# A place of its own for every step of a planned adapter kernel, and fourteen more W1 blocks by DMA

## The chip, the cores and the metric

The kernel runs on one core of a Trainium2 chip. The core has five engines, each with its own in-order queue: PE (TensorE, matrix products; its weight loads are listed as PEld), DVE (VectorE), ACT (ScalarE), POOL (GpSimd) and SP (SyncE, which here only issues DMAs). The metric is the device time of one execution in microseconds (us); less is better.

## The reference

128 batches of 128 x 512 floats, each with an id of one of ten "languages". A batch takes its own weights by its id, and passes through a small adapter, a layer norm and a residual:

```python
w1 = W1[ids]                                    # 512 x 128 per batch
w2 = W2[ids]                                    # 128 x 512
h = relu(einsum('bsh,bha->bsa', x, w1) + b1[ids])
y = x + einsum('bsa,bah->bsh', h, w2) + b2[ids]
normed = (y - mean(y)) * rsqrt(var(y) + 1e-5)
out = x + normed * gamma[ids] + beta[ids]
```

Everything is float32.

## The kernel before

W1 and W2 of all languages, and b2, gamma and beta spread over the 128 partitions, are loaded or made once at the start. After that each batch b passes through these steps, each a function of its own:

- SP: `load_x` (four batches in one DMA of 1 MB, four buffers, so sixteen batches), `store` (two batches, 512 KB). SP waits at a DMA until its data or its buffer is ready, with everything behind it in the queue.
- PE: `transpose_x` (four transposes, into the one PSUM buffer pxT), `down` (four products with W1, into the one PSUM buffer ph), `up` (the product with W2, into one of the five PSUM buffers py).
- ACT: `copy_xT` (pxT to SBUF), `stage_w1` (copies the batch's W1 from the loaded table), `relu` (ph to hT), `square` (sum of squares of py), and per pair of batches `scalar_means` and `deviation` (the root; L426).
- POOL: `add_b2` (r = x + b2) and `add_beta` (o = x + beta, in one of eight buffers of two batches).
- DVE: `residual` (py = py + r, with its sum), per pair three small Newton steps `rstd`, then `scale` (times gamma) and `finish` (o = py * rstd + o). The finish frees the buffer of py.

Batches differ in two ways. A letter of KINDS says how b2 and x get in. P: r is made by POOL. E ("seeded"): ACT copies x into py beforehand (`seed`), the product is added onto it (L367), and DVE adds b2 from its table; POOL then has one add less. "-" stands for the older forms in the first and last batches (b2 by a product, or by an extra DVE add). A letter of TURNS says how W1 and the transposed x come. T: by `stage_w1` and `transpose_x`. w: W1 by id from HBM (`load_late`, a DMA of 256 KB in pieces of 512 bytes), x by `transpose_x`. F: both in 32 x 32 blocks by DMA (`load_rows`, `load_blocks`), turned on DVE (`turn_blocks`, L302); such a batch has no `transpose_x` and no `copy_xT`.

The order of all this is a plan: each step of each batch is put down with a due time, in units of a batch, and the plan is sorted. Before, the due times are b plus one offset per step (BATCH, PAIR), with a second set (BATCH_EDGE, EDGE) for the "-" batches. KINDS and TURNS repeat every sixteen batches, KINDS from batch 26 and TURNS from batch 32 on. The sorted order becomes the order of each engine's queue; `keep` ties every instruction behind the one before it on its engine. Buffers are handed out in the sorted order too, the one that was freed longest ago first. The opening up to `x_turn(4)` stands ahead of the plan; the last steps (E is 123: products from batch 119 on, finishes from 116 on) are written out by hand behind it and use the same functions.

Of the kernel before, what the change touches and what calls it, by code (L numbers as in the profile page):

```python
# [22 lines left out]
U = 2  # L23
MIDDLE = 26
TURNED = 32
LAST = 4
# [5 lines left out]
BATCH_EDGE = dict(copy=0.2, r=0.05, r_late=1.05, beta=1.06, relu=1.3, w1=-0.6, up=2.5)  # L32
SEED = {'E': 1.69}
PAIR = dict(stat=0.22, square=0.34, means=1.98, root=1.9, scale0=3.03, n1=2.43, n2=3.115, n3=3.28, scale1=3.4, end0=3.67, end1=4.32)
EDGE = dict(stat=0.6, square=0.68, means=1.75, root=1.77, scale0=2.64, n1=2.65, n2=3.592, n3=3.62, scale1=3.64, end0=3.66, end1=4.66)
# [3 lines left out]
def cond_resid_kernel(ctx: ExitStack, tc: tile.TileContext, x, itok, W1, b1, W2, b2, gamma, beta, out):  # L39
# [225 lines left out]
    def b2_by_matmul(b):  # L265
        return b in (0, 1) or b >= B - 2

    def kind(b):
        return KINDS[b % len(KINDS)] if MIDDLE <= b < B - LAST else "-"

    def turn(b):
        return TURNS[b % len(TURNS)] if TURNED <= b < B - LAST - 2 else "-"

# [3 lines left out]
    def b2_on_gpsimd(b):  # L277
        return kind(b) in ON_GPSIMD or kind(b) == "-" and not b2_by_matmul(b) and not b2_by_vector(b)

    def b2_by_vector(b):  # L280
        return kind(b) == "-" and (b in (2, 3, 9, 13, 17, 21) or 24 <= b < B - 8 and (b % 16 in (1, 6, 11) or b % 32 == 30))
# [127 lines left out]
    def square(b):  # L409

        g, j = divmod(b, 2)
        if j == 0:
            ssqs[g] = st.tile([P, 2], FP, tag="ssq", name=f"ssq_{g}")
# [236 lines left out]

    for b in range(B):
        when = BATCH_EDGE if kind(b) == "-" else BATCH
        if b >= 20 and b % G == 0:
            at((11 if b == 20 else b - 7) - 0.01, load_x, b // G)
# [4 lines left out]
        if turn(b) in "Fw":  # L659
            at(b + BATCH["load"] - 1, lid, b, ET.SP)  # L660
            at(b + BATCH["load"], load_rows if turn(b) == "F" else load_late, b)
        if turn(b) == "F":
            at(b + BATCH["load"], load_blocks, b)
            at(b + BATCH["turn"], turn_blocks, b)
        elif 5 <= b <= E - 2:
            at(b, transpose_x, b)
            at(b + when["copy"], copy_xT, b)
        if 4 <= b <= E - 3:
            at(b + (when["r"] if seeded(b) else when["r_late"]), add_b2, b)
            at(b + when["beta"], add_beta, b)  # L670
            at(b + 1.1, down, b)
            at(b + when["relu"], relu, b)
        if seeded(b):
            at(b + SEED[kind(b)], seed, b)
        if FIRST <= b <= E - 1 and turn(b) not in "Fw":
            at(b + when["w1"], stage_w1, b)
        if 2 <= b <= E - 4:
            at(b + when["up"], up, b)
# [4 lines left out]
    def at_pair(g, when, step, *args):  # L683
        if g < E // 2 - 3 or (step, *args) in begun:
            at(2 * g + 3 + when, step, *args)

    for g in range(E // 2 - 1):
        b = 2 * g
        when = EDGE if "-" in (kind(b), kind(b + 2)) else PAIR
        for j in (0, 1):  # L690
            at_pair(g, j + when["stat"] - 0.01, vector_b2, b + j)
            at_pair(g, j + when["stat"], residual, b + j)
            at_pair(g, j + when["square"], square, b + j)
        at_pair(g, when["means"], scalar_means, g)
        at_pair(g, when["root"], deviation, g)
        if b % G == 0 and on(b + G):
            at_pair(g, when["end0"] + 0.001, lid, b + G, ET.DVE)
        for n in (1, 2, 3):
            at_pair(g, when[f"n{n}"], rstd, g, n)
        for j in (0, 1):  # L700
            at_pair(g, when[f"scale{j}"], scale, b + j)
# [194 lines left out]
```

## Time and profile before

| | us |
|---|---|
| median of three runs | 301.42 |
| the three runs | 300.8, 301.42, 1073.14 |
| the profiled run: its time | 301.23 |
| the profiled run: its span, first to last instruction | 298.8 |

The profile is of one execution. A row of "busy time by stretch" gives a stretch's start and end, its length, then the busy time (and count) of PE, PEld, DVE, ACT and POOL, the granted TensorE clock (1.00 is full), the mean busy share of the sixteen DMA engines, and GB/s. A row of the chain of waits gives start, length, engine, tile, line and count: at each moment the work that what comes last had to wait for. A row of the timeline gives start, length, engine, line, operation, out<-in, and in brackets the idle time before it with what ended it. A row of a group ends with total busy us, mean ns of one, and idle us before. In these rows DVE's and ACT's instructions can overlap their neighbours by some hundredths of a us. Tiles: pxT, xT, ph, hT, py as above; w1s is a batch's W1, w the tables of W1 and W2, b_b, gamma_b, beta_b the spread vectors.

| engine | main instructions, mean ns each |
|---|---|
| DVE | residual 690, scale 753, finish 748, turn 703, Newton step 150 |
| ACT | square 690 and 209 for its sum, copy_xT 580, stage_w1 623, relu 372, seed 599, root 266 |
| POOL | add 1306 |

### The profile page before, as it was taken

How to read it: one execution, taken by the hardware profiler on the slowest of the kernel's cores; microseconds unless marked ns; L12 is line 12 of the kernel's file. 1: busy time of each engine (PE TensorE's matmuls, PEld its weight loads, DVE VectorE, ACT ScalarE, POOL GpSimd, SP SyncE). 2: the span in 40 equal slices, each digit the busy share in tenths (PEclk: the TensorE clock that was granted, in tenths of full speed). 3: DMA queues.
4: the chain of work that ended last, by engine and by line, in shares of the span. 5: the costliest groups of instructions: out<-in, count | busy, mean ns of one | idle time of the engine just before them, and what ended most of it. 6: DMA issues, size and time to landing. Idle time of an engine off the chain costs nothing.

```text
span 298.8 us, 7251 instructions
## 1 busy us (share of the span) xinstructions
PE 290.7 (97%) x1783; PEld 214.7 (72%) x1783; DVE 288.9 (97%) x775; ACT 277.2 (93%) x766; POOL 277.4 (93%) x233
## 2 busy tenths in 40 slices
PE   7899999999999999999999999999999999999993
PEld 3758777777777777777777777777777777777761
DVE  6989999999999999999999999999999999999995
ACT  5868789999999999999999999999999999999983
POOL 1299998999999999999999999999999999999962
PEclk9999999999999999999999999999999999999998
DMA  6999999996799697988888887898988698894715
GB/s 233 369 393 370 342 329 396 400 325 212 270 297 328 169 378 218 321 316 284 277 280 295 275 283 256 281 300 224 356 256 269 233 313 301 250 349 163 237 73 219
DMA packets 61195, 85.48 MB, mean 286 GB/s; under 512 B 3641, under 2 KB 25156, under 8 KB 61154
## 3 DMA queue, kind: packets, MB, share of 16 engines
q1 hardware_dynamic: 61094, 84.97, 85.1%
q8 instruction: 15, 0.25, 0.3%
q14 instruction: 26, 0.21, 0.2%
q10 hardware_dynamic: 60, 0.05, 0.1%
HBM read 51.45 MB, written 33.55 MB: 284 GB/s over the span
## 4 chain that ended last, share of the span: by engine, by line
PE 81%; DVE 6%; ACT 4%; DMA 3%; issue 3%; SPq 1%; DVEq 0%; POOL 0%; ACTq 0%; POOLq 0%
PE ph L353 33%; PE py L375 26%; PE pxT L330 15%; PE py L367 7%; DMA w<-in_L_cond_W_dram 3%; DVE py L393 2%; ACT sq L416 1%; DVE o L553 1%; DVE py L459 1%; ACT w1s L321 1%; ACT xT L334 1%; SPq L173 1%; DVE n L559 0%; ACT hT L361 0%; ACT root L426 0%
## 5 line engine op out<-in xcount | busy, mean ns | idle before, releaser
L347 POOL TENSOR_TENSOR o<-x,beta_b 128x512 f32<-128x512 f32 x121 | 155.8, 1306 | 12.9 <-DVE beta_b L259 11.6
L353 PE MATMUL ph<-xT,w1s 128*128 128x128 f32 x1024 | 136.4, 276 | 0.1
L353 PEld LDWEIGHTS ph<-xT,w1s 128*128 128x128 f32 x1024 | 125.0, 192 | 8.7 <-ACT hT L361 7.0
L340 POOL TENSOR_TENSOR r<-x,b_b 128x512 f32<-128x512 f32 x89 | 116.1, 1305 | 0.0
L375 PE MATMUL py<-w,hT 128*128 x208 | 106.7, 595 | 0.7 <-DMA w<-in_L_cond_W_dram 0.7
L330 PEld LDWEIGHTS pxT<-ident,x 128*128 128x128 f32 x468 | 60.4, 150 | 60.6 <-issue 41.6
L459 DVE SCALAR_TENSOR_TENSOR py<-py,nmean,gamma_b 128x512 f32<-128x512 f32 x124 | 93.3, 753 | 0.0
L468 DVE SCALAR_TENSOR_TENSOR o<-py,rstd,o 128x512 f32<-128x512 f32 x116 | 86.8, 748 | 0.0
L416 ACT ACTIVATE sq<-py,sum 128x512 f32<-128x512 f32 x124 | 85.6, 690 | 0.7 <-DVE rstd L435 0.2
L334 ACT COPY xT<-pxT 128x512 f32<-128x512 f32 x117 | 67.8, 580 | 6.0 <-PE pxT L330 5.8
L330 PE MATMUL pxT<-ident,x 128*128 128x128 f32 x468 | 71.2, 275 | 0.9 <-ACT gamma_b L244 0.7
L393 DVE SCALAR_TENSOR_TENSOR py<-py,r 128x512 f32<-128x512 f32 x94 | 64.9, 690 | 1.4
L321 ACT COPY w1s<-w 128x512 f32 x91 | 56.7, 623 | 0.0
L361 ACT ACTIVATE hT<-ph,b1T 128x128 f32<-128x128 f32 x128 | 47.6, 372 | 5.1 <-PE ph L353 3.4
L375 PEld LDWEIGHTS py<-w,hT 128*128 128x128 f32 x208 | 31.7, 192 | 2.1 <-DMA w<-in_L_cond_W_dram 1.2
L416 ACT ACTIVATION_READ_ACCUMULATOR sq<-py,sum 128x1 f32 x124 | 25.9, 209 | 0.0
L367 PE MATMUL py<-w,hT 128*128 x48 | 25.3, 610 | 0.0
L393 DVE SCALAR_TENSOR_TENSOR py<-py,b_b 128x512 f32<-128x512 f32 x24 | 16.6, 693 | 1.5 <-PE py L367 1.4
L426 ACT ACTIVATE root<-ssq,eps 128x2 f32<-128x2 f32 x62 | 16.5, 266 | 1.5
L316 ACT COPY py<-x 128x512 f32<-128x512 f32 x24 | 14.4, 599 | 0.0
L393 DVE DVE_READ_ACCUMULATOR py<-py,r 128x1 f32 x94 | 13.2, 140 | 0.0
L407 ACT ACTIVATE nmean<-sum 128x2 f32<-128x2 f32 x61 | 11.7, 192 | 0.0
(79 smaller groups left out, 139.8 us busy)
## 6 DMA issues: line engine op xcount, KB each, us to landing
out_dram<-o SPq DMA_DIRECT2D x62, 512.0 KB, 4.0
x<-in_x_dram SPq DMA_DIRECT2D x27, 1024.0 KB, 7.7
w1s<-in_L_cond_W_dram SPq DMA_DIRECT2D x26, 256.0 KB, 7.3
x<-in_x_dram SPq DMA_DIRECT2D x10, 512.0 KB, 6.0
w1s<-in_L_cond_W_dram SPq DMA_DIRECT2D x44, 64.0 KB, 3.2
x<-in_x_dram SPq DMA_DIRECT2D x44, 64.0 KB, 2.1
w<-in_L_cond_W_dram SPq DMA_DIRECT2D x4, 640.0 KB, 8.1
w<-in_L_cond_W_dram SPq DMA_DIRECT2D x1, 1792.0 KB, 10.2
```

Source lines behind the costliest of these rows:

```text
L321: keep(nc.scalar.copy(w1s[b].rearrange("p k a -> p (k a)"), src))
L330: keep(nc.tensor.transpose(pxs[b][:, k, :], cols, ident))
L334: keep(nc.scalar.copy(xT[b], pxs.pop(b)))
L340: keep(nc.gpsimd.tensor_tensor(rs[b], xb(b), b2_b[:, bass.ds(v * H, H)], ALU.add))
L347: keep(nc.gpsimd.tensor_tensor(os[g][:, j, :], xb(b), beta_b[:, bass.ds(v * H, H)], ALU.add))
L353: nc.tensor.matmul(phs[b], lhsT=w1s[b][:, k, :], rhs=xT_of(b, k), start=(k == 0), stop=(k == KC - 1))
L361: keep(nc.scalar.activation(hT[b], phs.pop(b), AF.Relu, bias=b1T[:, bass.ds(lid(b, ET.Activation), 1)]))
L375: keep(nc.tensor.matmul(ys[b], lhsT=hT[b], rhs=w2[:, bass.ds(v * H, H)], start=not m, stop=True))
L393: nc.vector.scalar_tensor_tensor(ys[b], ys[b], 1.0, r, ALU.mult, ALU.add, accum_out=sum_of(b))
L416: nc.scalar.activation(sq, ys[b], AF.Square, bias=col(sums, b), scale=-float(H), accum_out=col(ssqs, b))
L459: nc.vector.scalar_tensor_tensor(ys[b], ys[b], col(nmeans, b), gamma_b[:, bass.ds(v * H, H)], ALU.add, ALU.mult)
L468: nc.vector.scalar_tensor_tensor(o, ys[b], rstds[g][:, j : j + 1], o, ALU.mult, ALU.add)
```

## The change

The due times come from a table, STEPS: for each step 32 numbers for the first 32 batches, 16 for the steady ones (used by b modulo 16, batches 32 to 111) and 16 for the last ones. X_STEPS does the same for the loads of x from group 5 on. KINDS and TURNS become three strings each, in the same way, which now hold the older forms too (M: b2 by a product, D: by DVE).

- The kinds of all batches stay as they are except that the seeded batch 118 becomes 114.
- F stays at the same eleven batches. W1 by id (w) goes from batches 41, 57, 73, 89, 105 and 121 to three in each steady sixteen (b modulo 16 is 1, 3 or 10) and five in the last sixteen: 33, 35, 42, 49, 51, 58, ... 106, 113, 114, 117, 120, 121. `stage_w1` is left out for these.
- Every engine's queue gets another order. On ACT most roots stand behind another step than the square they need, and `scalar_means` is often ahead of them. On DVE the two scales or the two finishes of a pair are sometimes swapped and a finish can stand behind the next residual. On POOL `add_b2` tends to be earlier and `add_beta` of many batches some places later. On SP stores are put later, and some behind stores of later pairs.
- `add_beta` and `square` take a new buffer when their pair has none yet, whichever of the two batches comes first.

```diff
-KINDS = 'EPPPPPEPEPPPEPPP'
-TURNS = 'TTTTFTTTTwTTFTTT'
+KINDS = ('MMDDPPPPPDPPPDPPPDPPPDPPPPPPEPPP', 'EPPPPPEPEPPPEPPP', 'EPEPPPPPEPPPPPMM')
+TURNS = ('TTTTTTTTTTTTTTTTTTTTTTTTTTTTTTTT', 'TwTwFTTTTTwTFTTT', 'TwwTFwTTwwTTTTTT')
...
-BATCH = dict(turn=0.19, copy=0.16, r=-0.36, beta=-0.13, relu=1.26, w1=-0.77, up=2.66, load=-5.59, r_late=0.22)
...
-SEED = {'E': 1.69}
-PAIR = dict(stat=0.22, square=0.34, means=1.98, root=1.9, scale0=3.03, n1=2.43, n2=3.115, n3=3.28, scale1=3.4, end0=3.67, end1=4.32)
...
+STEPS = {
...
+    "seed": (
...
+        (1.87, 0, 0, 0, 0, 0, 2.12, 0, 1.65, 0, 0, 0, 1.84, 0, 0, 0,),
+        (1.72, 0, 2.81, 0, 0, 0, 0, 0, 17.54, 0, 0, 0, 0, 0, 0, 0,),
+    ),
...
+    "root": (
...
+        (5.62, 0, 5.22, 0, 5.16, 0, 5.5, 0, 5.55, 0, 5.01, 0, 5.32, 0, 5.85, 0,),
...
+    "store": (
...
+        (13.59, 0, 10.32, 0, 16.57, 0, 12.81, 0, 11.43, 0, 10.29, 0, 16.68, 0, 10.53, 0,),
+        (21.95, 0, 23.89, 0, 0, 0, 0, 0, 0, 0, 0, 0, 0, 0, 0, 0,),
+    ),
+}
+X_STEPS = (-7.52, -2.84, -5.71, -5.13, -7.35, -7.96, -7.38, -5.13, -7.35, -7.96, -7.38, -5.13, -7.35, -7.96, -7.38, -5.13, -7.35, -7.96, -7.38, -5.13, -7.35, -7.96, -7.38, -6.83, -1.57, -5.91, -2.19)
...
+    def of(parts, b):
+        if b < len(parts[0]):
+            return parts[0][b]
+        return parts[1][b % steady] if b < closing else parts[2][b - closing]
...
-        if j == 0:
+        if g not in os:
             os[g] = op.tile([P, 2, H], FP, tag="o", name=f"o_{g}")
...
+    def when(name, b):
+        return b + of(STEPS[name], b)
...
         if seeded(b):
-            at(b + SEED[kind(b)], seed, b)
+            at(when("seed", b), seed, b)
         if FIRST <= b <= E - 1 and turn(b) not in "Fw":
-            at(b + when["w1"], stage_w1, b)
+            at(when("w1", b), stage_w1, b)
...
-        at_pair(g, when["root"], deviation, g)
+        at_pair(g, when("root", b), deviation, g)
...
-        at_pair(g, when["end1"] + 0.001, store, g)
+        at_pair(g, when("store", b), store, g)
```

More of the change, by code (lines that the diff above doesn't have):

```diff
@@ L665, in cond_resid_kernel @@
         elif 5 <= b <= E - 2:
-            at(b, transpose_x, b)
-            at(b + when["copy"], copy_xT, b)
+            at(when("transpose", b), transpose_x, b)
+            at(when("copy", b), copy_xT, b)
         if 4 <= b <= E - 3:
[L669 to L672, printed above, removed]
+            if b2_on_gpsimd(b):
+                at(when("r", b), add_b2, b)
```

100 lines of the change are left out of this document (65 added, 35 removed), and 68 rows, old and new, of the table STEPS.

## The prediction

> **What bounds the kernel now.** I read the page's first part, then busy time by stretch, then the chain of waits over one group of sixteen batches, then the timeline around a seeded batch. The page shows every engine almost full, so none of its shares names the bound:
>
> ```profile
> span 298.8 us, 7251 instructions
> PE 290.7 (97%) x1783; PEld 214.7 (72%) x1783; DVE 288.9 (97%) x775; ACT 277.2 (93%) x766; POOL 277.4 (93%) x233
> 20.00:53.00 33.00, 33.00 (x211) 25.76 (x211) 32.45 (x85) 28.04 (x81) 31.71 (x27) 1.00 1.09 363
> 88.80:123.39 34.59, 34.59 (x218) 25.87 (x217) 34.22 (x92) 34.04 (x96) 34.59 (x29) 1.00 0.87 281
> ```
>
> The last two rows are stretches: length, then busy time of PE, PEld, DVE, ACT, POOL, then granted clock, DMA share, GB/s; the last one is a group of sixteen batches, 34.59 us. The clock is full, PE and POOL have no gap, DVE 0.4. What a group costs is read from the chain, which runs on PE alone here:
>
> ```profile
> 118.85 0.44 PE pxT L330 x4
> 119.28 0.89 PE ph L353 x8
> 120.18 1.02 PE py L367 x2
> 121.20 0.44 PE pxT L330 x4
> 121.64 0.89 PE ph L353 x8
> 122.53 0.86 PE py L375 x2
> 123.39 0.97 PE ph L353 x8
> ```
>
> An undisturbed batch is four transposes 0.44, `down` 0.89, `up` 0.86: 2.19 us. A batch of turn F has no transposes (123.39 follows an `up` at once): 1.75. Sixteen batches with two F are 14 x 2.19 + 2 x 1.75 = 34.16 us of pure PE work, so PE loses 0.43 us per group, in steps like the 0.16 of the seeded product at 120.18 (1.02 for 0.86) and the 0.08 at 123.39 (0.97 for 0.89). One of them from near:
>
> ```profile
> 154.19 0.60 ACT L316 COPY py<-x 128x512 f32<-128x512 f32 x1
> ...
> 154.85 1.13 PE L367 MATMUL py<-w,hT 128*128 x2
> ...
> 156.01 0.70 DVE L393 SCALAR_TENSOR_TENSOR py<-py,b_b 128x512 f32<-128x512 f32 x1 [0.17 <-PE py L367]
> ```
>
> `seed` on ACT ends at 154.79 and the product starts right behind it, at 154.85; `copy_xT`, queued behind the seed, makes the next step late too. ACT is what makes PE late, and DVE then waits 0.17 for the product. That is all there is to win: 0.43 per group, over batches 32 to 121 (5.6 groups) 2.4 us, under 1% of the time.
>
> **The change, part by part.** Counted in the order of the built program, PE, DVE and POOL get exactly the same instructions: 11 F, 24 seeds (118 becomes 114), 89 adds of b2, as many of beta. Only two things differ: which batches get W1 by DMA (20 batches with turn w, 6 before), and the order in each queue.
>
> *W1 by DMA.* Fourteen copies leave ACT, two per group of sixteen and four in the last one.
>
> ```profile
> L321 ACT COPY w1s<-w 128x512 f32 x91 | 56.7, 623 | 0.0
> ```
>
> ```profile
> L582 SPq DMA_DIRECT2D w1s<-in_L_cond_W_dram x9: 376/395/395, 88.7 to 276.2; - x9
> ...
> DMA to landing us min/median/max: 3.4/3.8/4.2
> L83 SPq DMA_DIRECT2D x<-in_x_dram x27: 379/413/1322, 42.0 to 262.3; - x27
> ...
> DMA to landing us min/median/max: 6.3/7.7/12.5
> ```
>
> ACT goes from 34.04 to 34.04 - 2 x 0.62 = 32.8 us per group, 1.4 below PE's 34.16. Its copies were hidden as long as PE was slower; what they cost was the lateness above. Walking ACT's new order past PE's 2.19 steps (inputs of ACT ready when PE's rows end), every `copy_xT`, `relu` and `seed` is done before PE asks for it; the tightest are the seed of batch 6 of each group, about 0.0, and `relu` of batch 7, about 0.1. The root behind another step than its square takes a wait out of ACT's queue, hidden there. On the DMA side two loads of 256 KB per group are 0.52 MB in 34.6 us, 15 GB/s on top of 281; the stretch 20 to 53 carried 363. Price on the path: nothing, as long as they land in time (rival C).
>
> *DVE's order.* Same work. From one instruction's start to the next:
>
> ```profile
> 149.39 0.69 DVE L393 SCALAR_TENSOR_TENSOR py<-py,r 128x512 f32<-128x512 f32 x1
> 150.00 0.14 DVE L393 DVE_READ_ACCUMULATOR py<-py,r 128x1 f32 x1
> 150.00 0.15 DVE L435 SCALAR_TENSOR_TENSOR rstd<-part,root 128x2 f32<-128x2 f32 x1
> 150.07 0.75 DVE L459 SCALAR_TENSOR_TENSOR py<-py,nmean,gamma_b 128x512 f32<-128x512 f32 x1
> 150.74 0.75 DVE L468 SCALAR_TENSOR_TENSOR o<-py,rstd,o 128x512 f32<-128x512 f32 x1
> ```
>
> ```profile
> L302 DVE STREAM_TRANSPOSE xT<-x 128x512 f32<-128x512 f32 x11 | 7.7, 703 | 0.0
> ```
>
> residual 0.61, Newton step 0.07, scale 0.67, each about 0.08 less than its row's length, since neighbours overlap. For finish (0.75 long, as scale) I take 0.66, for the turn 0.70 - 0.08 = 0.62. A group: 16 x (0.61 + 0.67 + 0.66) + 24 x 0.07 + 2 x 0.62 = 33.96 us, 0.20 under PE's 34.16. So DVE keeps up if its order makes it wait no more than 0.2 per group. What ties PE to DVE is the five buffers of py: a product needs the finish of an earlier batch. In the built program each product takes the buffer that was freed longest ago, so the swapped finishes do not collide: product 77 gets the buffer of 73, not of 72, whose finish now stands behind residual 76. Walked from residual 64 (which starts as product 64 ends) to residual 80, DVE falls at most 1.2 us behind PE, and the closest release is 0.55 us early (finish 64 for product 69). Cost nothing, with that 0.55 as cover.
>
> *POOL's order.* 28 adds per group.
>
> ```profile
> 156.12 1.30 POOL L340 TENSOR_TENSOR r<-x,b_b 128x512 f32<-128x512 f32 x1
> 157.35 1.30 POOL L347 TENSOR_TENSOR o<-x,beta_b 128x512 f32<-128x512 f32 x1
> 158.58 1.29 POOL L340 TENSOR_TENSOR r<-x,b_b 128x512 f32<-128x512 f32 x1
> ...
> 160.69 0.69 DVE L393 SCALAR_TENSOR_TENSOR py<-py,r 128x512 f32<-128x512 f32 x1
> ```
>
> ```profile
> 47.68 2.51 POOL L347 TENSOR_TENSOR o<-x,beta_b 128x512 f32<-128x512 f32 x2 [1.29 <-DMA out_dram<-o]
> ```
>
> One add each 1.23 us, 34.44 per group: POOL is 0.28 slower than PE's pure work and lives on its lead. The first row and the one of DVE are the sum r of batch 66 (POOL's 116th add) and its use: 160.69 - 157.42 = 3.3 us of lead. In the new order it stands one place later, 2.0; nearly all other r stand earlier. POOL's one wait, 1.29 for the first store, shrinks to 0.06, since the add that takes that buffer is now its 29th and not its 28th, 1.23 later. With that, 3.3 again; PE running 0.34 per group faster eats 1.9 us by batch 120, and the lead stays above 1. The late beta adds (up to seven places later) keep 2.6 us or more before their finish outside the first 25 batches; in those, r of 20 and 25 are within 0.5 of their use without the saved wait and 1.2 better with it. Cost nothing, at worst 0.5.
>
> *SP's order.* Stores now stand out of turn, behind or ahead of loads; SP waits at a store until its finish, with all loads behind it waiting too. The x loads are planned 5 to 8 batches (11 to 17 us) ahead, against the 7.7 above, except those of batches 116 to 119 and 124 to 127, planned 1.6 and 2.2 ahead. What counts is when SP comes to them: the buffer of the former is free after POOL's 189th add, 73 places behind the 116th at 156.12, so at 156.12 + 74 x 1.23 = 247.1, and they are first transposed here:
>
> ```profile
> 263.58 0.60 PE L330 MATMUL pxT<-ident,x 128*128 128x128 f32 x4
> ```
>
> 16 us later, more than the longest 12.5. Cost nothing, except for W1 in the last sixteen batches, rival C.
>
> **Sum.** The profiled run took 301.23 us, 2.4 beyond its span; the median of the three was 301.42. Of PE's 0.43 per group I let 0.34 go (what remains, 0.1, is the tight seed and `relu`): 0.34 x 5.6 = 1.9. First batches and the hand-written end, which keep their instructions: nothing. 301.2 - 1.9 = **299.3 us**. Bounds: all 2.4, the saved POOL wait of 1.3 beside it if POOL should have held the end, give 298.8 and 297.5; none gives 301.2.
>
> **Rivals.**
>
> A, POOL paces (15%). If POOL's lead is used up, a group takes 34.44 plus small gaps, about 34.5, 0.09 better than now: 301.2 - 0.5 = 300.7. For: POOL never idles in the rows by stretch. Against: the 3.3 us of lead. That the change does nothing (PE's order of steps is almost the same) lands at the same place.
>
> C, the last loads come late (13%). W1 of batch 121 is now issued at the end of SP's plan, behind the store of pair 55, x of the last four batches and the store of pair 54.
>
> ```profile
> 265.05 0.74 DVE L468 SCALAR_TENSOR_TENSOR o<-py,rstd,o 128x512 f32<-128x512 f32 x1
> ...
> 274.97 1.06 PE L353 MATMUL ph<-xT,w1s 128*128 128x128 f32 x8
> ```
>
> Finish 111 ends at 265.8 (first row); three issues of 0.4 later the load goes out at 267.0, and `down` of 121 stands at 275.0: 8 us, against 3.4 to 4.2. No stall. But if it can only land behind the 1 MB of x issued 0.8 earlier, which takes 6.3 to 12.5, PE stalls between 0 and 3.7 us, and with 0.9 for its own bytes at 300 GB/s up to 4.6: 299.3 + 3 = 302.3, at most 303.9. [...] No trace here has a small load right behind an x load, so it is open.
>
> D, DVE falls behind and the buffers of py hold PE (7%). It has 0.2 us per group in hand, and the new order puts residuals sooner behind their product (the 0.17 above is such a wait). If each of the eight pairs costs 0.25 of waiting, a group takes 33.96 + 2.0 = 35.96, 1.37 more than now, over 5.6 groups +7.7: 308.9. From 0.22 per pair on it is more than 2% slower. Against it: the walk, in which DVE waits only at the seeded residual 64.
>
> **How the numbers follow.** Forecast 62%, A 15%, C 13%, D 7%; 3% for what I do not see. A measurement of this kernel tells about 2%, 6 us, from no change. Faster by that would need 295.2, under every bound above: 1%. Slower: D and half of the unseen, 8%. Within: 91%. The range for 8 in 10 begins between the two lower bounds, at 298.2, and takes in A and most of C, to 303.2.
>
> **What would show it.** Right: in the chain, seeded products at 0.86 like the others and about 34.2 to 34.4 us per sixteen batches; ACT under 33 of them; 77 copies of W1 and 23 loads of it by id in the steady program; POOL without its 1.3 wait; DVE still the same busy time. Wrong: POOL waiting on nothing while DVE waits on r (A); `down` of 121 or 117 waiting for a DMA (C); PE waiting for DVE at an `up` (D).

## The result, and the profile after

The changed kernel takes 314.5 us, median of four runs (311.75 to 315.75), beside 301.1 for the kernel before: a ratio of 1.0435, 95% interval 1.0342 to 1.0529. It is slower by some 13 us; the prediction said 299.3 with a range up to 303.2. Here and below a median is over all runs of a kernel, and a ratio leaves out the runs of the slow state (one each of x_behind_blocks and steady_in_turn). The page of its profiled run, the first part, and from the last part the DMA issues (a row ends with count, KB each, and the median us from issue to landing):

```profile
span 313.5 us, 7282 instructions
PE 295.9 (94%) x1783; PEld 217.9 (70%) x1783; DVE 289.6 (92%) x775; ACT 270.6 (86%) x752; POOL 277.5 (89%) x233
...
x<-in_x_dram SPq DMA_DIRECT2D x27, 1024.0 KB, 11.1
...
w1s<-in_L_cond_W_dram SPq DMA_DIRECT2D x44, 64.0 KB, 7.9
x<-in_x_dram SPq DMA_DIRECT2D x44, 64.0 KB, 5.2
```

The same rows of the DMA issues before:

```profile
x<-in_x_dram SPq DMA_DIRECT2D x27, 1024.0 KB, 7.7
...
w1s<-in_L_cond_W_dram SPq DMA_DIRECT2D x44, 64.0 KB, 3.2
x<-in_x_dram SPq DMA_DIRECT2D x44, 64.0 KB, 2.1
```

The loads of x take 3.4 us longer, the pieces of 64 KB (an F batch has four of W1 and four of x) more than twice as long. DVE and POOL work as long as before, ACT 6.6 us less, PE by its modelled ends 5.2 more (some of it at half clock, as told below); the span has grown by 14.7 us, and every engine idles in it. Whom they wait for is in the view of waits (engine, tile, line, what ended the wait; then us in total, times, longest). Five of its rows, all new but the second, which was 1.3 us in one wait before, are:

```profile
DVE xT L414 <- DMA x<-in_x_dram: 8.9, 4, 3.9
POOL o L459 <- DMA out_dram<-o: 6.4, 4, 2.2
POOL o L459 <- DMA x<-in_x_dram: 4.2, 1, 4.2
POOL r L452 <- DVE py L505: 2.5, 1, 2.5
PE pxT L442 <- DMA x<-in_x_dram: 3.5, 1, 3.5
```

Four of the five name a DMA: blocks of x for an F batch that DVE is to turn, stores that have not given back their o buffer, x loads. The same view for SP alone shows the queue behind them; before, its largest waits were 100.7 us in 35 waits at stores for DVE, and only 1.6 us at the blocks for an x load:

```profile
SPq L402 <- DMA x<-in_x_dram: 35.6, 10, 4.2
SPq L584 <- DVE part L544: 16.9, 7, 10.9
```

L402 issues the x blocks of an F batch, L584 the stores. The timeline of SP up to the first F batch (36), after and then before (start, us, line, out<-in, count):

```profile
63.23 4.75 SPq L584 DMA_DIRECT2D out_dram<-o  x2
68.08 0.41 SPq L187 DMA_DIRECT2D x<-in_x_dram  x1
68.55 1.56 SPq L584 DMA_DIRECT2D out_dram<-o  x2
70.22 0.75 SPq L187 DMA_DIRECT2D x<-in_x_dram  x1
71.58 3.13 SPq L694 DMA_DIRECT2D w1s<-in_L_cond_W_dram  x2
74.82 3.13 SPq L584 DMA_DIRECT2D out_dram<-o  x2
78.60 0.39 SPq L187 DMA_DIRECT2D x<-in_x_dram  x1
79.25 4.56 SPq L408 DMA_DIRECT2D w1s<-in_L_cond_W_dram  x4
83.94 6.72 SPq L402 DMA_DIRECT2D x<-in_x_dram  x4
```

```profile
75.49 0.37 SPq L472 DMA_DIRECT2D out_dram<-o  x1
76.12 3.07 SPq L296 DMA_DIRECT2D w1s<-in_L_cond_W_dram  x4
79.31 1.78 SPq L290 DMA_DIRECT2D x<-in_x_dram  x4
81.19 0.41 SPq L472 DMA_DIRECT2D out_dram<-o  x1
81.70 0.41 SPq L83 DMA_DIRECT2D x<-in_x_dram  x1
```

After, SP stands at one late store until 63.23 (10.9 us, the longest wait above), and then sends out what has gathered: six stores, three x loads and two W1 loads, 6.8 million bytes in the 15.8 us to 78.99, or 432 GB/s. In the same 15.8 us the DMA engines moved 252 GB/s, so what stands in the queue grows. The x load of 78.60 goes out directly ahead of the eight DMAs of batch 36, and the last of the four blocks, at 90.35, goes out 6.4 us after the first. Before, the eight follow a store, and the x load comes behind them. DVE, and the chain of waits over the same time (start, length, work):

```profile
88.40 0.15 DVE L542 SCALAR_TENSOR_TENSOR part<-ssq,root 128x2 f32<-128x2 f32 x1
92.42 0.71 DVE L414 STREAM_TRANSPOSE xT<-x 128x512 f32<-128x512 f32 x1 [3.87 <-DMA x<-in_x_dram]
```

```profile
78.60 11.73 DMA x<-in_x_dram
...
90.35 1.90 DMA x<-in_x_dram
...
95.22 0.62 DVE o L580
...
95.88 1.13 PE py L487 x2
```

The chain reads: the x load lands after 11.7 us, only then goes the last block out, 1.9 us later it is there, DVE (idle for 3.87 us, at the turn, with everything queued behind it) comes to the finish that frees a py buffer, and PE can go on. F batches 68, 84 and 100 repeat this with waits of 1.82, 1.32 and 1.94; together with the 3.87 they are the 8.9 of the waits.

The other loss is in the last sixteen batches. The x load of batches 116 to 119 goes out at 263.83 and lands 9.5 us later. PE stands for it at the transposes of 117, and POOL for the load in front of it:

```profile
268.88 1.02 PE L487 MATMUL py<-w,hT 128*128 x2
273.45 1.09 PE L442 MATMUL pxT<-ident,x 128*128 128x128 f32 x4 [3.55 <-DMA x<-in_x_dram]
274.33 1.91 PE L465 MATMUL ph<-xT,w1s 128*128 128x128 f32 x8
```

```profile
270.26 1.27 POOL L459 TENSOR_TENSOR o<-x,beta_b 128x512 f32<-128x512 f32 x1 [4.17 <-DMA x<-in_x_dram]
```

The rows of PE hold more than the wait. From 272.84 to 276.25 the granted clock was 0.50 in this trace, and PE works slowly through it: the four transposes took 1.09 us, where the next four took 0.60, and the eight products of `down` 1.91, where the next eight took 1.05. By an estimate from that clock, half of the 2.8 us from 273.45 to 276.25, 1.4 us, is lost on top of the 3.55; the two groups are 0.49 and 0.86 longer than the next ones.

Where PE stands can be told batch by batch: the start of the first product of `down`, in the trace of a run, minus the same in the trace of before, both counted from the start of the span. Below it stands so for all runs (told in the next section), in us later (minus: earlier), with POOL's idle time between the first and the last of its planned adds, the end of the last of them, and the span:

```
                       down of batch                                    POOL
run                      32    37    53    69    85   101   112   122   idle   last   span
before                    0     0     0     0     0     0     0     0    1.3  273.3  298.8
the change             0.45  3.75  3.68  4.62  5.59  7.90  8.12 14.55   13.8  287.0  313.5
sp_in_turn             0.48  0.30 -0.12 -0.29 -0.36 -0.41 -0.23  7.05   13.0  285.0  311.0
fewer_w1_loads         0.71  1.58  1.75  1.77  1.96  1.83  2.06  2.83    6.0  278.2  302.1
before_more_w1        -0.34 -0.58 -0.82 -1.19 -1.22 -1.45 -1.45 -1.25    0.1  273.3  298.0
before_sp_late        -0.14  0.08  0.93  0.76  0.78  0.80  0.81  0.82    0.1  273.3  299.7
x_behind_blocks        0.34  0.10 -0.05 -0.53  0.68  2.29  2.25  9.62   10.4  282.7  308.6
rows_x_blocks          0.61  2.33  2.08  1.60  1.59  1.81  2.41  3.87    5.2  277.5  302.8
blocks_first           0.52  2.64  2.57  2.03  2.28  4.95  5.01 12.48   13.8  286.2  311.4
x29_sooner             0.75  3.32  3.16  3.67  4.08  6.38  6.82 12.14   15.0  288.2  312.2
closing_fewer_w1       0.69  2.79  2.54  2.07  3.28  6.20  6.32  7.68    9.6  283.1  306.8
steady_in_turn         1.04  0.83  0.54  0.48  0.44  0.49  0.72 11.30    9.7  282.8  310.2
other_orders           0.57  0.85  0.64  0.43  0.22  0.47  0.29  1.86    7.5  279.8  305.2
in_turn_and_closing    0.85  0.70  0.92  1.05  0.76  0.79  1.08  3.24    8.0  281.2  306.5
nine_o_buffers         0.11  2.56  2.54  2.08  2.08  4.43  4.90 11.16   11.9  284.1  310.1
beta_120_later         0.91  2.66  2.56  2.24  3.95  6.10  6.17 10.74   10.0  283.3  309.7
one_add_more          -0.04  0.03  0.02 -0.04  1.06  2.21  3.29  4.15    0.2  280.6  304.4
one_add_less          -0.27  0.14  0.81  1.29  2.00  2.66  2.92  4.06    5.1  269.8  303.3
add_less_even_10       0.35  0.11  0.00 -0.29 -0.39 -0.50 -0.37  1.28    3.0  268.9  300.6
add_less_even_2       -0.02 -0.13 -0.22 -0.52 -0.63 -0.74 -0.74 -0.43    0.6  266.3  298.8
```

So the change loses 0.45 by batch 32, 3.4 around F 36, 1.0 to 1.5 at each of F 68, 84 and 100, 0.9 at batch 97 (its cause stays open), and 6.4 in the closing. Of the 6.4, 3.55 are PE's wait for x, 1.4 the half clock, and 1.0 come at `down` of 121, which waits for its W1. F 52, where DVE does not wait, costs nothing (3.68 at 51 and 53).

### The profile page after: what moved, and what is told of

It is laid out like the page before. It is cut to its first block, busy times and chain, and to the rows that moved or that the text cites. A ratio compares the mean times of both kernels' runs of the same rounds, so it can differ in the third digit from the quotient of the medians.

```text
span 313.5 us, 7282 instructions
## 1 busy us (share of the span) xinstructions
PE 295.9 (94%) x1783; PEld 217.9 (70%) x1783; DVE 289.6 (92%) x775; ACT 270.6 (86%) x752; POOL 277.5 (89%) x233
## 4 chain that ended last, share of the span: by engine, by line
PE 39%; DMA 16%; POOL 14%; DVE 13%; issue 13%; ACT 1%; POOLq 1%; DVEq 1%; SPq 0%; ACTq 0%
DMA x<-in_x_dram 15%; PE ph L465 15%; PE py L487 13%; PE pxT L442 7%; POOL r L452 7%; POOL o L459 7%; DVE py L505 5%; DVE o L580 3%; DVE py L571 2%; PE py L479 2%; PE row L345 1%; DVE o L665 1%; POOLq L259 1%; DMA rows<-in_L_cond_b_dram 1%; DVEq L259 1%
## 5 line engine op out<-in xcount | busy, mean ns | idle before, releaser
L459 POOL TENSOR_TENSOR o<-x,beta_b 128x512 f32<-128x512 f32 x121 | 152.2, 1292 | 23.2 <-DVE beta_b L363 12.7
L465 PEld LDWEIGHTS ph<-xT,w1s 128*128 128x128 f32 x1024 | 127.3, 193 | 22.0 <-ACT hT L473 11.3
L452 POOL TENSOR_TENSOR r<-x,b_b 128x512 f32<-128x512 f32 x89 | 112.5, 1292 | 3.2 <-DVE py L505 2.5
L580 DVE SCALAR_TENSOR_TENSOR o<-py,rstd,o 128x512 f32<-128x512 f32 x116 | 84.8, 746 | 0.7
L442 PE MATMUL pxT<-ident,x 128*128 128x128 f32 x468 | 72.3, 278 | 3.5 <-DMA x<-in_x_dram 3.5
L446 ACT COPY xT<-pxT 128x512 f32<-128x512 f32 x117 | 69.0, 589 | 6.4 <-PE pxT L442 6.1
L433 ACT COPY w1s<-w 128x512 f32 x77 | 46.9, 626 | 1.0 <-issue 1.0
L414 DVE STREAM_TRANSPOSE xT<-x 128x512 f32<-128x512 f32 x11 | 7.8, 705 | 8.9 <-DMA x<-in_x_dram 8.9
## 6 DMA issues: line engine op xcount, KB each, us to landing
x<-in_x_dram SPq DMA_DIRECT2D x27, 1024.0 KB, 11.1
```

The source lines that it names most:

```text
L433: keep(nc.scalar.copy(w1s[b].rearrange("p k a -> p (k a)"), src))
L442: keep(nc.tensor.transpose(pxs[b][:, k, :], cols, ident))
L446: keep(nc.scalar.copy(xT[b], pxs.pop(b)))
L452: keep(nc.gpsimd.tensor_tensor(rs[b], xb(b), b2_b[:, bass.ds(v * H, H)], ALU.add))
L459: keep(nc.gpsimd.tensor_tensor(os[g][:, j, :], xb(b), beta_b[:, bass.ds(v * H, H)], ALU.add))
L465: nc.tensor.matmul(phs[b], lhsT=w1s[b][:, k, :], rhs=xT_of(b, k), start=(k == 0), stop=(k == KC - 1))
```

## The experiments

Each ratio is to the kernel before on the same chip, with its 95% interval. The numbers of a diff are due times in batches, as in the change.

### The order on SP, or the bytes

**sp_in_turn**: the change with SP's old due times.

```diff
 "load" (F and w, batches 32 to 127)
-  -3.21, -5.7, -1.63, -4.11, -5.92, -6.32, ...
+  -5.59
 "store"
-  13.59, 10.32, 16.57, ...
+  0.001 behind the later finish of the pair
-X_STEPS = (-7.52, -2.84, -5.71, -5.13, ...)
+X_STEPS = (-9.01, -7.01, -7.01, -7.01, ...)
```

> The changed kernel with SP's due times of the kernel before: each store right behind its pair's last finish, in turn, F and W1 loads 5.59 batches ahead, x loads 7.01 ahead. W1 loads, DVE, POOL, ACT and PE orders stay those of the changed kernel. Theory R (SP's order is the whole loss, in the last sixteen batches too): SP waits at the stores again, the ring is short, no turn waits for its blocks: 298 to 301 us. Theory O: the loss is in the other queues, 310 or more. Theory B: 308 or more, since all W1 loads are still there.

313.57 us, ratio 1.0436 (1.0406 to 1.0467). By this number alone R falls, but where the time is lost tells another tale. Up to batch 112 PE is 0.23 us ahead of before: in the steady batches the whole loss is gone, with all W1 loads and all other new orders in place. From there to the end of the span it loses 12 us; POOL waits:

```profile
256.63 1.31 POOL L459 TENSOR_TENSOR o<-x,beta_b 128x512 f32<-128x512 f32 x1
268.98 1.26 POOL L459 TENSOR_TENSOR o<-x,beta_b 128x512 f32<-128x512 f32 x1 [11.04 <-DMA x<-in_x_dram]
```

The second row is the beta of batch 120. In the new order POOL makes it ahead of the r of 116, so it wants the x load of 120 to 123 before it goes on with 116 to 119; in turn, SP brings that load second, behind the blocks of 116, a store and a W1 load. My expectation had not looked at what POOL's new order asks of SP in the closing.

**fewer_w1_loads**: the turns of before in the change (`stage_w1` 0.77 ahead for the fourteen, and the loads that stay 5.59 ahead; that of 121 stood 11.31 behind).

```diff
-TURNS = ('T...T', 'TwTwFTTTTTwTFTTT', 'TwwTFwTTwwTTTTTT')
+TURNS = ('T...T', 'TTTTFTTTTwTTFTTT', 'TTTTFTTTTwTTTTTT')
```

> The changed kernel with the turns of the kernel before: W1 by id only in batches 41, 57, 73, 89, 105 and 121, the other fourteen copied by ACT again (0.77 of a batch ahead, as before); all other places as in the changed kernel. Theory B (the added bytes are the cause): back to 300 to 302 us. Theory R: the two W1 loads ahead of each of F 36, 52, 68, 84, 100 are 0.5 MB, 1.4 us of ring; the waits of 3.9, 1.8, 1.3, 1.9 become about 2.5, 0.4, 0, 0.5, and the x load of batches 116 to 119 comes about 1 us earlier: 308 to 310 us.

303.79 us, 1.0099 (1.0078 to 1.0121): between the two theories, nearer to B. Without the fourteen loads 10.7 of the 13.4 us are gone, though SP's order is still the new one. DVE waits only once, 1.28 at F 36. And SP waits even longer than in the change at the blocks for an x load, 43.6 us for 35.6:

```profile
SPq L402 <- DMA x<-in_x_dram: 43.6, 16, 4.7
```

So that wait of SP's is not by itself what costs.

**before_more_w1**: the other way round, the W1 loads alone, in the kernel before.

```diff
-TURNS = 'TTTTFTTTTwTTFTTT'
+TURNS = 'TwTwFTTTTTwTFTTT'
```

> The kernel before with the changed kernel's steady turns: W1 by id in three of sixteen batches (33, 35, 42, 49, ... 113, 115), seventeen loads for six, all 5.59 batches ahead, SP in turn as before. Theory R (order, not bytes): 300.5 to 301.5 us, as the kernel before. Theory B (DMA engines at 0.87 busy have no room for 0.52 MB more in a group): 304 or more, DVE's turns waiting for their blocks.

300.02 us, 0.9981 (0.9969 to 0.9992), as R said, and 0.2% under the kernel before. With SP in turn the added bytes land in time, though DMA is busier than it was (0.87 to 0.90 in this stretch; start:end, us, busy PE, PEld, DVE, ACT, POOL, clock, DMA share, GB/s), and ACT is at 33.5 where it was at 34.0:

```profile
88.80:123.39 34.59, 34.59 (x221) 26.09 (x220) 34.43 (x92) 33.51 (x94) 34.59 (x29) 1.00 0.90 276
```

**before_sp_late**: SP's new places alone, for batches 32 to 111.

```diff
+LOAD = {4: -3.21, 12: -5.7}
+STORE = (13.59, 10.32, 16.57, 12.81, 11.43, 10.29, 16.68, 10.53)
+X_LOAD = (-5.13, -7.35, -7.96, -7.38)
...
-        at_pair(g, when["end1"] + 0.001, store, g)
+        at_pair(g, STORE[g % 8] - 3 if 16 <= g < 56 else when["end1"] + 0.001, store, g)
```

> The kernel before, its own W1 turns, with the changed kernel's places on SP for batches 32 to 111: stores late and out of turn, x loads directly ahead of the F batches' eight DMAs, F loads 3.21 and 5.70 batches ahead and not 5.59. Theory R: F 36 waits for its blocks as in the run with fewer W1 loads (1.3 us), the other turns not; 302 to 304 us. If the order alone were the whole loss: 308 or more.

301.60 us, 1.0030 (1.0009 to 1.0051): DVE waits 0.35 at the turn of F 36, by the profile for an `up` of PE and not for the blocks, and not at all at the others; a little less than R had.

Together: the loads alone -0.2%, SP's order alone +0.3%, the change, which has both and the new orders of the four other queues, +4.4%. In the steady batches it takes the two: from batch 32 to 112 PE loses 7.7 us in the change, 1.4 without the added loads, and wins 0.7 with SP in turn. SP's order leaves little time between a transfer's issue and its use (3.21 batches for every second F batch, 5.59 before), and the loads lengthen what stands ahead of it (W1 by id took 8.9 us to land in the change, 3.8 before). The two together in the kernel before, without the new orders of the other queues, were not run.

### Why the blocks come late

**x_behind_blocks**: five x loads moved behind the eight DMAs.

```diff
 X_STEPS, groups 10, 14, 18, 22, 26
-  -7.96
+  -7.2
```

> The changed kernel, but the x loads of groups 10, 14, 18, 22 and 26, which stand on SP directly ahead of the eight DMAs of F batches 36, 52, 68, 84 and 100, stand directly behind them. Theory R (what stands ahead in SP's ring lands first): the blocks have 1 MB less ahead of them, 2.9 us at 350 GB/s; DVE's four waits at the turns (3.9, 1.8, 1.3, 1.9 us) shrink to about 1 for batch 36 and 0 for the others, so about 307 to 308 us. Theory B (the added W1 DMAs take the bandwidth; the order does not matter): the same bytes at the same time, no more than 1 us gained, 313 to 315. Theory O (the loss comes from the new order of DVE, POOL or ACT): unchanged, 314.

309.73 us, 1.0246 (1.0208 to 1.0283). R's 350 GB/s is an estimate: the change moved 360 GB/s from 20 to 53 us, and 284 over its whole span. The four waits of DVE are gone altogether, and PE is 0.53 us ahead of before at batch 69, 5.2 better than the change. Some 2 us more than R said are lost later: 2.8 between batches 69 and 112, where POOL waits for stores (3.1 us in three waits), and 7.4 in the closing, where PE waits 4.6 us for x and the clock is 0.50 for 6.8 us.

**rows_x_blocks**: the same, and the blocks a little behind.

```diff
-            at(when("load", b), load_blocks, b)
+            at(when("load", b) + 0.02, load_blocks, b)
 X_STEPS, groups 10, 14, 18, 22, 26
-  -7.96
+  -7.2
```

> The changed kernel, but in all F batches the x load next to them stands between the four W1 blocks and the four x blocks, so that the DMA eight places ahead of the last x block is a store or a W1 load, no longer the x load. Theory S (SP issues a DMA only when the DMA eight places ahead of it has landed, and this wait for the x load is what makes the last block late): the waits at the turns go, 307 to 308 us. Theory R (the ring lands DMAs in the order of issue): the blocks still land behind the 1 MB of x, DVE still waits 1 to 4 us at the turns of 36, 68, 84 and 100, and the time stays at 313 to 316.

304.87 us, 1.0136 (1.0100 to 1.0171). What the edit does is less than the expectation says: it puts the x load between rows and blocks in F 36, 52, 68, 84 and 100; in 44, 60, 76, 92 and 108 it still stands ahead of all eight. Accordingly SP's waits at the blocks for x are five, not ten:

```profile
SPq L402 <- DMA x<-in_x_dram: 15.9, 5, 3.6
```

and DVE still waits at F 36, not at the others:

```profile
91.00 0.71 DVE L414 STREAM_TRANSPOSE xT<-x 128x512 f32<-128x512 f32 x1 [2.53 <-DMA x<-in_x_dram]
```

S foretold none of these waits, R all four: neither is the whole, and the time is below what either had. The closing, where nothing was edited, loses 1.5 us and not 6.4. SP comes to the x load of 116 to 119 at 255.01, 8.8 us earlier than in the change, while PE at batch 112 is only 5.7 us earlier.

**blocks_first**: no x load moved, the blocks ahead of the W1 rows.

```diff
-            at(when("load", b), load_rows if turn(b) == "F" else load_late, b)
+            at(when("load", b) + 0.001 * (turn(b) == "F"), load_rows if turn(b) == "F" else load_late, b)
```

> The changed kernel, but in each F batch the four DMAs of x blocks stand ahead of the four of W1; the x load in front of all eight stays. So the DMA eight places ahead of the last x block is no longer the x load (it is now that of the last W1 part), but the blocks still stand behind its 1 MB. Theory S (SP waits until the DMA eight places ahead has landed, and this makes the blocks late): DVE's waits at the turns (3.9, 1.8, 1.3, 1.9 us) go, about 307 us. Theory R (the ring lands in order of issue, so they land right behind the x load in any case): only the last block's own 1.0 to 1.9 us goes; waits of about 2.7, 0.7, 0.2 and 0.8, and 310 to 313 us.

312.95 us, 1.0400 (1.0368 to 1.0433), and DVE's waits are 2.70, 0, 0.15 and 0.72, where R had 2.7, 0.7, 0.2 and 0.8. Of DVE's 8.9 us at the turns 3.6 are left, behind the 1 MB of x. The 1.2 to 1.8 us that each wait lost are two things at once: the wait for the x load eight places ahead, and the 256 KB of W1 rows, which now stand behind the blocks; this run does not part them. With the x load behind (x_behind_blocks) none of the waits is left. In no run did a DMA land out of turn: in each of the twenty traces every one of SP's DMAs whose landing is complete (239 of 241 in the change, 225 of 227 before) landed after the one issued before it.

### The closing

**x29_sooner**: the x load of 116 to 119 three places earlier.

```diff
 X_STEPS, group 29
-  -1.57
+  -6.31
```

> The changed kernel with one number changed: the x load of batches 116 to 119 stands directly behind the blocks of F batch 116, ahead of the W1 load of 113 and the x load of 120 to 123, and no longer behind both. Theory R (the ring lands in order of issue, and PE's 4.35 us wait at the transposes of 117 is this load's place): 1.25 MB less ahead of it, 3.6 us at 350 GB/s, so 310 to 312 us. Theory P (POOL adds beta of batch 120 ahead of r of 116, so it needs the other x load first): POOL waits that much longer and the gain is lost, 313 to 316.

314.32 us, 1.0441 (1.0406 to 1.0476): nothing won, as P said. POOL's wait for the other x load grows from 4.2 to 7.7, and PE now waits for the W1 of 113 (3.5 us; this load had stood behind it) and of 117 (1.6):

```profile
POOL o L459 <- DMA x<-in_x_dram: 7.7, 1, 7.7
...
PE ph L465 <- DMA w1s<-in_L_cond_W_dram: 5.1, 2, 3.5
```

Here, what came earlier for one transfer came later for those that it passed.

**closing_fewer_w1**: 113, 114, 117 and 120 copied by ACT.

```diff
-TURNS = (..., 'TwTwFTTTTTwTFTTT', 'TwwTFwTTwwTTTTTT')
+TURNS = (..., 'TwTwFTTTTTwTFTTT', 'TTTTFTTTTwTTTTTT')
 "load" of batch 121
-  11.31
+  -5.59
```

> The changed kernel, but W1 of batches 113, 114, 117 and 120 copied by ACT again; only 121 stays a load in the last sixteen. All steady batches as changed. Theory R: 1 MB less in SP's ring around the x load of 116 to 119; the loss in the closing shrinks from 6.4 us to 1 to 3 us: 309 to 311 us. If the closing is lost to POOL's or DVE's order instead: 314.

308.56 us, 1.0280 (1.0239 to 1.0320). The closing loses 1.4 us instead of 6.4. The edit does two things: it takes 1 MB of W1 from around the x loads, and it puts the load of 121 ahead, which takes away the 1.0 us at `down` of 121. So some 4 of the 5.0 us go with the 1 MB; among them are the 1.4 of the half clock: in this closing PE's longest wait is 1.2 us, and the clock stays at 1.00 until its products are done.

**steady_in_turn**: SP in turn for batches 32 to 111 only, and for the closing

```diff
 X_STEPS, groups 29, 30
-  -1.57, -5.91
+  -6.31, -9.3
```

> The changed kernel with SP in turn for batches 32 to 111 alone (stores behind their finish, F and W1 loads 5.59 ahead, x loads 7.01 ahead); in the last sixteen the changed kernel's own places, but the x loads of 116 to 119 and of 120 to 123 both right behind the blocks of F 116, the second earlier than in the in-turn run, where POOL waited 11.0 us for it. Theory R: nothing lost in the steady batches (0.5 us won by batch 118, as in that run), 1 to 2 us lost in the closing: 301 to 303 us. Theory B (the W1 loads of the closing, 113, 114, 117, 120 and 121, are its loss): 305 or more.

309.93 us, 1.0302 (1.0280 to 1.0323). 0.72 at batch 112, then 10.6 lost, B's case: the W1 of 113 and 117 land behind the x loads and hold PE for 7.2 us, while POOL waits for x all the same. Beside each of the two waits the clock is 0.50 for 3.4 us, some 3 us of the loss by the estimate made for the change:

```profile
POOL o L459 <- DMA x<-in_x_dram: 8.7, 1, 8.7
...
PE ph L465 <- DMA w1s<-in_L_cond_W_dram: 7.2, 2, 4.6
```

**in_turn_and_closing**: this, with the turns of closing_fewer_w1.

```diff
-TURNS = (..., 'TwTwFTTTTTwTFTTT', 'TwwTFwTTwwTTTTTT')
+TURNS = (..., 'TwTwFTTTTTwTFTTT', 'TTTTFTTTTwTTTTTT')
 "load" of 121 as in closing_fewer_w1
 "load", "store", X_STEPS as in steady_in_turn
```

> As the run with the steady batches in turn on SP and the x loads of 116 to 123 early, and W1 of 113, 114, 117 and 120 by ACT; the three W1 loads in each steady sixteen stay. Theory R: that run lost 10.5 us in its closing, with W1 of 113 and 117 landing late behind the x loads; without them the closing loses no more than 1.5: 301 to 303 us. If the closing's loss has another cause (POOL waiting 8 us for x): 308 or more.

307.32 us, 1.0202 (1.0167 to 1.0237). PE's loss in the closing shrinks to 2.2, as R had it, but the end does not follow: POOL waits 7.4 us for the beta of 120, and the program ends 26 us behind `down` of 122, where all but this run, sp_in_turn and other_orders have 21.7 to 23.1.

**other_orders**: this, with the steady turns of before too. Left of the change are the orders of PE, ACT, DVE and POOL, and SP's places in the opening and the closing.

```diff
-TURNS = (..., 'TwTwFTTTTTwTFTTT', 'TwwTFwTTwwTTTTTT')
+TURNS = (..., 'TTTTFTTTTwTTFTTT', 'TTTTFTTTTwTTTTTT')
 "load" of 121 as in closing_fewer_w1
 "load", "store", X_STEPS as in steady_in_turn
```

> The changed kernel's orders of PE, ACT, DVE and POOL, but W1 by DMA only where the kernel before has it, and SP in turn for batches 32 to 111 (the x loads of 116 to 123 right behind the blocks of 116). What is left of the change is the order of the four other queues. If my steps on DVE and POOL hold (they cost nothing): 300.5 to 302 us. If these orders lose time by themselves: 303 or more.

307.25 us, 1.0225 (1.0203 to 1.0246): time is lost, but not in the steady batches. From batch 32 to 112 PE gains 0.28, so the new orders cost nothing there; and they win next to nothing. In the closing POOL again waits at the beta of 120:

```profile
263.73 1.28 POOL L459 TENSOR_TENSOR o<-x,beta_b 128x512 f32<-128x512 f32 x1 [5.24 <-DMA x<-in_x_dram]
```

### What sets the end

In the sixteen runs with 210 planned adds on POOL, the last of them ends at the start of the first plus POOL's idle time plus 258.9 to 259.3 us. So its adds took 1.23 us each in all of them, and what POOL loses in waits it does not make good. That made POOL, not PE, the suspect.

**nine_o_buffers** and **beta_120_later**, on the change:

```diff
-    op = ctx.enter_context(tc.tile_pool(name="op", bufs=8))
+    op = ctx.enter_context(tc.tile_pool(name="op", bufs=9))
```

```diff
 "r" of batch 115, "beta" of 113, 114, 115 (due 118.05 to 118.12; beta of 120 is due 118.16)
-  3.18   5.48, 6.56, 5.42
+  3.05   5.10, 4.12, 3.11
```

> The changed kernel with nine buffers of two batches for o, not eight. Theory POOL (POOL's adds run back to back and pace the program; it lost 6.4 us in four waits of 0.9 to 2.2 us for a store to release its o buffer): these go, about 308 us. Theory PE (PE paces; it lost 8.1 us at F batches and 6.4 in the closing, and waits of POOL lie beside it): DVE's waits at the turns are unchanged, no gain, 313 to 315.

> The changed kernel with POOL's adds r of 115 and beta of 113, 115 and 114, whose x has long landed, ahead of beta of 120, the first add that needs one of the last two x loads and waited 4.2 us for it. SP and PE as in the changed kernel. Theory POOL: 4 us less, 310 to 311 us, though PE still waits some 4 us for x at the transposes of 117. Theory PE: that wait sets the end, 313 to 315.

311.54 us, 1.0357 (1.0334 to 1.0379), and 311.97, 1.0387 (1.0344 to 1.0430): 3.0 and 2.5 us below the median of the change, between the two theories. The four runs of the change lie 4 us apart, and its interval holds both ratios, so by the times alone neither gain is sure. The first takes all of POOL's waits for stores away, the second its wait for x, but in each the other waits stay or grow (5.4 for x in the first; 2.9 more for a store in the second), and PE still loses 6.3 and 4.6 in the closing.

**one_add_more** and **one_add_less**, on the kernel before (the second with the turns of before_more_w1):

```diff
-KINDS = 'EPPPPPEPEPPPEPPP'
+KINDS = 'EPPPPPPPEPPPEPPP'
```

```diff
-KINDS = 'EPPPPPEPEPPPEPPP'
+KINDS = 'EPPEPPEPEPPPEPPP'
```

> The kernel before with the seeded batch 6 of each sixteen made a P batch (38, 54, 70, 86, 102, 118): POOL gets one add of 1.23 us more for each of the six, ACT one seed of 0.6 less, PE and DVE the same work. Theory POOL: 6 x 1.23 = 7.4 us more, 308 us. Theory PE (POOL has 3.3 us of lead and PE's 34.6 a group is the pace): PE loses less at the seeds, 300 to 301 us, or a few us more once the lead is gone, at most 304.

> The kernel before with W1 by id in three of sixteen batches (as in the run before_more_w1, 300.0 us) and one more seeded batch, 3 of each sixteen (35, 51, 67, 83, 99, 115): POOL has one add of 1.23 us less for each of these six, ACT 0.6 more. Theory POOL: POOL 33.4 us a group, PE's 34.2 is then the pace, 0.4 a group under 34.6: 2 us less, 297.5 to 298.5 us. Theory PE: as before_more_w1, 300.

One add more: 306.15 us, 1.0186 (1.0166 to 1.0206), between the two theories. PE keeps its old pace to batch 69, and then loses some 1 us per sixteen. That fits a lead of 3.3 us that the first groups use up: of the 7.4 us more, 4.1 are left, and PE is 4.15 late at batch 122. From there POOL is the pace. One add less: 305.19, 1.0157 (1.0136 to 1.0177), slower, against both theories. POOL ends 3.5 us earlier than before, and PE 4.1 later: the seed of batch 35, an odd one, waits for a py buffer, and everything behind it on ACT with it. The same 0.51 us stand at each of the six added seeds, and PE loses some 0.65 at each:

```profile
91.02 0.59 ACT L316 COPY py<-x 128x512 f32<-128x512 f32 x1 [0.51 <-DVE o L468]
```

**add_less_even_10** and **add_less_even_2**: the fifth seed at an even batch, otherwise as one_add_less.

```diff
-KINDS = 'EPPPPPEPEPPPEPPP'
+KINDS = 'EPPPPPEPEPEPEPPP'
```

```diff
-KINDS = 'EPPPPPEPEPPPEPPP'
+KINDS = 'EPEPPPEPEPPPEPPP'
```

> The kernel before with W1 by id in three of sixteen batches and a fifth seeded batch, 10 of each sixteen (42, 58, 74, 90, 106), whose W1 comes by DMA: POOL 27 adds a group, 33.3 us. If the seed finds its py buffer free, PE sets the pace at 34.2 to 34.4: 298.5 to 299.7 us, a little below the 300.0 of before_more_w1. If a seed holds up PE there too, 0.65 for each of five: 302 to 303 us.

> As the other run, with the fifth seeded batch at 2 of each sixteen (34, 50, 66, 82, 98, 114), where ACT also copies W1: 298.5 to 300 us if the seed's buffer is free; 302 to 304 if PE waits 0.65 at each of six.

For 10 of each sixteen, 302.37 us, 1.0050 (1.0030 to 1.0070): PE is 0.5 ahead up to batch 121 and loses 1.8 at 122, for a cause that stays open. For 2 of each sixteen, 300.42, 0.9982 (0.9964 to 1.0000), no better than before_more_w1, though POOL is done 7 us earlier. So PE and POOL run at nearly one pace: with one add more POOL sets the end, and taking adds away from it wins nothing.

## Why the prediction was wrong

**The step that failed: SP's order, "Cost nothing, except for W1 in the last sixteen batches".** I walked the x loads and the W1 of 121, and nothing else that SP issues. In the steady batches this order, together with the added loads, cost PE 7.7 us, where with SP in turn PE gains 0.7. The eight DMAs of an F batch, moved from 5.59 batches ahead to 3.21 in every second one and put right behind an x load, were not walked at all, nor was any store's hold on its o buffer. And the x loads were walked with 7.7 us from issue to landing, taken from a queue in turn; in the new queue the median is 11.1, and that of a late W1 load, 3.4 to 4.2 before, is 8.9:

```profile
DMA to landing us min/median/max: 4.0/8.9/11.5
```

The x load of 116 to 119 I let go out when its buffer comes free, at 247.1; before, it went out at 244.29. In the change it went out at 263.83, since SP came to it only behind the eight DMAs of F 116, the W1 of 113 and the load of 120 to 123. (The x load of 24 to 27 is planned 2.84 ahead, which I had not listed either.) SP's waits at the stores, 100 us, had looked like idle time; where they are back (sp_in_turn) the steady batches lose nothing.

**W1 by DMA, "nothing, as long as they land in time", and 1.9 us won.** Right with SP in turn: before_more_w1 has PE 1.1 us ahead from batch 32 to 112, 0.22 per sixteen where I had taken 0.34, and 1.7 ahead at 119; of this, 0.7 is left at the end. In the new queue the condition fails, and there the loads, with the late place of the one of 121, are worth 10.7 us (fewer_w1_loads). I had put both prices in separate terms of a sum, at zero each; what counted was that both stand in SP's one queue, where each DMA landed after the one issued before it.

**Rival C, the last loads.** Its condition, that a small load lands only behind the 1 MB of x issued before it, is what the traces show (in the change the x load of 277.42 landed at 287.27, the store behind it at 288.58, the W1 load of 279.27 at 289.32); I gave it 13%. At its own place, W1 of 121, it cost 1.0 us (PE 13.45 behind at `down` of 120, 14.48 at 121), inside its 0 to 3.7: this load came 10.1 us after its issue, and `down` of 121 began at 289.45. (The view of waits names a `copy_xT` of ACT there, which ended 0.04 us later still; it is that of 122, which this product does not need.) I had not asked where else in the queue a load stands right behind 1 MB.

**PE as the bound, and rival A.** The 34.16 us of pure work per sixteen are right; steady batches do go faster when nothing is late (0.4 us per sixteen in x_behind_blocks, 0.34 to -0.53 between 32 and 69). But POOL, at the same pace, has a lead of only 3.3 us and no slack to win back, so each of its waits counts once that is gone. I wrote that its wait for stores would shrink from 1.29 to 0.06; it grew to 6.4, as stores stand 10 to 17 batches behind and their buffers with them, and nine_o_buffers has none of it.

**DVE's order, rival D.** The order costs nothing in the steady batches (other_orders). Yet what D described was seen, DVE holding PE at an `up` through the py buffers; its cause was a DMA that DVE's queue waited for.

**POOL's order, "at worst 0.5".** In the steady batches right. In the closing the beta of 120 ahead of the r of 116 asks for the load of 120 to 123 before PE asks for that of 116 to 119; in the four runs with SP back in turn POOL waited 5.2 to 11.0 us there.

**What would show it** named POOL without its 1.3 wait, and `down` of 121 or 117 waiting for a DMA; the first came out the other way, the second at the transposes of 117. A DVE turn waiting for its blocks was not on the list.

**The clock.** The prediction read it as full, which held up to the closing; the half clock behind PE's wait, 1.4 us, was in no term.

Not settled: how the 14.7 us divide between PE's waits and POOL's, and whether the new orders of the other four queues have a part in the steady loss. The r and py buffers tie the two, and taking POOL's waits for stores or for x away gave 3.0 and 2.5 us, which the spread of the change's runs does not make sure, of the 6.4 and 4.9 that they sum to.

## What to carry to other kernels

When a queue of transfers gets a new order, walk every transfer in it, with the time from issue to landing that the new queue will have, not the old one's (11.1 us here for an x load, 7.7 before): in these traces each load landed behind all that SP had sent before it. Two edits that cost nothing alone can share one queue, as SP's order and the added loads do here (+0.3% and -0.2% alone, +4.4% in the change, which has both and more); price them together. And where two engines run at one pace, look for the waits of both: here, taking POOL's away showed 3.0 and 2.5 us of 6.4 and 4.9, with most of PE's still there.

The kernel to keep is before_more_w1, the old orders with three W1 loads per sixteen: 300.0 us, 0.2% under the kernel before (interval 0.1 to 0.3%, on one chip).

## What the runs showed of the hardware

In the trace's records the landings of SP's DMAs stand on eight semaphores, which recur in turn (230 of the change's 241 have that of the DMA eight places ahead). In the twenty traces none went out before the one eight places ahead of it had landed (the closest 0.02 us after it, in the change as before). In the change the last x block of each of F 36 to 108 is held by the x load eight places ahead (35.6 us in ten waits, the longest 4.2), and goes out 0.02 us after that has landed. So in the change an x load stopped the queue eight DMAs later. Alone this cost little (fewer_w1_loads stood 43.6 us so, at 303.8).

Beside some of PE's waits the granted clock was 0.50: for 3.4 us in the change, beside a wait of 3.55, and for 6.8 us in x_behind_blocks, beside 4.62. Eight of the twenty traces show it before PE's last products, in the closing, beside or just behind waits of 1.96 to 4.66 us; waits of 2.89 (beta_120_later) and 3.46 us (x29_sooner) passed without it. What tells the two apart these traces do not show. In the change the wait cost PE some 1.4 us more than its 3.55, by the estimate above.

The DMA engines were at 0.97 busy with 307 GB/s in sp_in_turn, steady batches, without PE losing time there (PE busy 33.92 of 34.00):

```profile
193.00:227.00 34.00, 33.92 (x211) 25.10 (x209) 33.92 (x91) 32.03 (x92) 34.00 (x28) 1.00 0.97 307
```
